# Kronecker feed-forward stage: how the eight PSUM banks are shared, where the output spreads stand in the order, and which queues store the last group

## The chip, the cores and the metric

The kernel runs on one NeuronCore of a Trainium2 chip. The metric is the device time of one execution in microseconds (us); the figure of a version is the median of its runs. All times inside the kernel come from one execution taken by the hardware profiler and are counted from its first instruction.

## The reference

The kernel computes two layers of a "metaformer" on an input of 4 x 32 x 32 tokens with 384 channels, all in fp32. The first layer (an attention and a mixture of experts) and the convolution of the second layer are not touched by the change. What matters is the last step, the feed-forward block of the second layer, whose two weight matrices are Kronecker products:

```python
def _L1_ffn_ref(x, c_fc_1, c_fc_2, c_proj_1, c_proj_2):
    w_fc = jnp.kron(c_fc_1, c_fc_2)          # (1536 x 32) kron (1 x 12)
    w_proj = jnp.kron(c_proj_1, c_proj_2)    # (32 x 1536) kron (12 x 1)
    h = x @ w_fc.T
    h = jax.nn.gelu(h, approximate=False)
    out = h @ w_proj.T
    return out
...
t = t + _L1_ffn_ref(_ln_t(t), ...)
```

Because of the Kronecker form, the 384 channels of a token shrink to 32 sums over 12 channels each, these 32 become 1536 hidden values, Gelu is applied, the 1536 values become 32 again, and each of the 32 is spread over 12 channels with the weights `c_proj_2`. The result is added to the input of the block.

## The kernel before

The 4096 tokens are 32 tiles of 128 tokens. The class `Kron` works on groups of 16 tiles (`GT`), so there are two groups, g = 0 and g = 1. The hidden values are 12 blocks (`NF`, f = 0 to 11) of 128. `shrink` (VectorE) makes the 32 sums of each token, and `run` (L1979) does the rest. In `run`:

- `turn(g)` (L1992) transposes the 32 sums of the 16 tiles on TensorE, so that 128 partitions hold four sets q of 32 rows and 512 columns hold four blocks n of 128 tokens. The tile of a pair (n, q) is 4n + q. VectorE copies the result out of PSUM (L2000).
- `hidden(g, f)`, called **H(f)** below, makes four matmuls (L2007), one for each q. Each contracts 32 rows, so the four stand on different 32-row strips of the array. Each writes its own PSUM tile `ps_h` of one bank (128 x 512 fp32), and ScalarE applies Gelu to each (L2012), which gives four tiles `h` in SBUF. In the trace every fp32 matmul is two weight loads and two matmul records, so H(f) shows as x8.
- `back(g, f)`, called **B(f)** below, makes four matmuls (L2018), one for each q, with all 128 rows and 32 columns each. They add into the four quarters of one PSUM bank `ps_y`. After f = 11 VectorE copies `ps_y` to `yT` (L2024).
- `spread(g, n, q)`, called a **spread** below, makes one matmul (L2031) with 32 rows that spreads the 32 values of 128 tokens over 384 channels into one PSUM bank `ps_o`. VectorE adds the input of the block (L2036) and writes a tile `o`, and a DMA of 192 KB stores it to `out` (L2037, issued by SyncE, SP). The tiles `o` rotate through four buffers.

The eight banks of PSUM are divided as four for `ps_h`, one for `ps_y` and three for `ps_o`, where `turn` uses the `ps_o` banks too. A matmul that writes a rotating tile waits until the reader of the tile that last held the bank is done.

The order of the work is written in the loop at the end of `run`. For each f it is H(f), then B(f-1); in group 0 also `begin` and `shrink` for group 1 and, at f = 10, `turn(1)`. In group 1, for f = 2 to 9, two spreads of group 0 follow B(f-1), so the sixteen spreads of group 0 lie inside the loop of group 1. The sixteen spreads of group 1 come after B(11), at the end of the program. In this part the framework orders the instructions of TensorE, VectorE and ScalarE by their place in the program and by what is ready in its own estimate; in the trace of before, TensorE's order in `run` is the order of the text. After the stage the program ends with a branch on the value `unsafe` (L2161) and a closing exchange of all engines.

Of the kernel before, what the change touches and what calls it, by code (L numbers as in the profile page):

```python
# [10 lines left out]
FP = mybir.dt.float32  # L11
# [3 lines left out]
PSUM = bass.MemoryType.PSUM  # L15

P = 128
# [1897 lines left out]
class Kron:  # L1915
# [63 lines left out]
    def run(self, out):  # L1979
        nc, tc, A = self.nc, self.tc, self.A  # L1980
        NG_ = NT // self.GT
        with ExitStack() as ctx:
            hp = ctx.enter_context(tc.tile_pool(name="kf_h", bufs=10, reuse_waits="tile"))
            tp = ctx.enter_context(tc.tile_pool(name="kf_t", bufs=2, reuse_waits="tile"))
            op = ctx.enter_context(tc.tile_pool(name="kf_o", bufs=4, reuse_waits="tile"))
            ps_h = ctx.enter_context(tc.tile_pool(name="kf_ps_h", bufs=4, space=PSUM, reuse_waits="tile"))
            ps_y = ctx.enter_context(tc.tile_pool(name="kf_ps_y", bufs=1, space=PSUM, reuse_waits="tile"))
            ps_o = ctx.enter_context(tc.tile_pool(name="kf_ps_o", bufs=3, space=PSUM, reuse_waits="tile"))
            xrT, hs, py = [], {}, {}
            yT = {}  # L1990

            def turn(g):  # L1992
                ps = ps_o.tile([P, 512], FP, name="ps_x", tag="o")
                flat = self.xr[g].rearrange("p t a -> p (t a)")
                for n in range(self.QT):
                    nc.tensor.transpose(
                        ps[:, n * P : (n + 1) * P], flat[:, n * P : (n + 1) * P], self.net.ident
                    )
                t = tp.tile([P, 512], FP, name="xrT", tag="xrT")
                nc.vector.tensor_copy(t, ps)  # L2000
                xrT.append(t)

            def hidden(g, f):
                for q in range(4):
                    rows = slice(A * q, A * q + A)
                    ps = ps_h.tile([P, 512], FP, name="ps_h", tag="h")
                    nc.tensor.matmul(  # L2007
                        ps, lhsT=self.wf[rows, f * P : (f + 1) * P], rhs=xrT[g][rows, :],
                        start=True, stop=True,
                    )  # L2010
                    h = hs[g, f, q] = hp.tile([P, 512], FP, name="h", tag="h")
                    nc.scalar.activation(h, ps, AF.Gelu)  # L2012

            def back(g, f):
                if f == 0:
                    py[g] = ps_y.tile([P, 512], FP, name="ps_y", tag="y")
                for q in range(4):
                    nc.tensor.matmul(  # L2018
                        py[g][A * q : A * q + A, :], lhsT=self.wp[:, f, :], rhs=hs.pop((g, f, q)),
                        start=f == 0, stop=f == NF - 1, skip_group_check=True,  # L2020
                    )
                if f == NF - 1:
                    yT[g] = tp.tile([P, 512], FP, name="yT", tag="yT")
                    nc.vector.tensor_copy(yT[g], py[g])  # L2024

            def spread(g, n, q):

                rows = slice(A * q, A * q + A)
                i = g * self.GT + 4 * n + q
                ps = ps_o.tile([P, 512], FP, name="ps_o", tag="o")  # L2030
                nc.tensor.matmul(  # L2031
                    ps[:, :C], lhsT=yT[g][rows, n * P : (n + 1) * P],
                    rhs=self.wide[rows, :, :].rearrange("p a k -> p (a k)"), start=True, stop=True,
                )
                o = op.tile([P, C], FP, name="o", tag="o")
                nc.vector.tensor_tensor(o, ps[:, :C], self.net.x(i), ALU.add)  # L2036
                nc.sync.dma_start(out=out[i * P : (i + 1) * P, :], in_=o)  # L2037

            turn(0)
            for g in range(NG_):  # L2040
                for f in range(NF):
                    hidden(g, f)
                    if f:
                        back(g, f - 1)
                    elif g:
                        back(g - 1, NF - 1)
                    if g + 1 < NG_:
                        if f == 0:
                            self.begin(g + 1)
                        if 1 <= f < 9:  # L2050
                            self.shrink(g + 1, 2 * f - 2)
                            self.shrink(g + 1, 2 * f - 1)
                        if f == 10:
                            turn(g + 1)
                    if g and 2 <= f < 10:
                        for q in range(2):
                            spread(g - 1, (f - 2) // 2, 2 * (f % 2) + q)
            back(NG_ - 1, NF - 1)
            for n in range(self.QT):
                for q in range(4):  # L2060
                    spread(NG_ - 1, n, q)


def gates(net, psum, gate_w, gate_b):
# [170 lines left out]
```

## Time and profile before

| what | us |
|---|---|
| median of three runs | 2975.26 (2974.44 to 2985.27) |
| the profiled execution's own time | 2946.74 |
| its span, first to last instruction | 2945.0 |
| H of group 0, f = 0 starts at | 2850.76 |
| H of group 1, f = 0 starts at | 2887.63 |
| last B of group 1 done, `yT` copied from | 2924.43 |
| last add of the program (L2036) from | 2937.22 |

The profiled execution is 28.5 us below the median of the runs without a profile. Times within the trace are compared with each other; a difference found there is then carried over to the median.

How to read what follows: a line of the timeline has the start in us, the duration in us, the engine (PE is TensorE's matmul, PEld its weight load, DVE is VectorE, ACT is ScalarE, SP is SyncE), the line, the operation, what is written from what, the shapes and the count of merged instructions. A bracket at the end says how long that engine was idle before it, and what released it.

### The profile page before, as it was taken

How to read it: one execution, taken by the hardware profiler on the slowest of the kernel's cores; microseconds unless marked ns; L12 is line 12 of the kernel's file. 1: busy time of each engine (PE TensorE's matmuls, PEld its weight loads, DVE VectorE, ACT ScalarE, POOL GpSimd, SP SyncE). 2: the span in 40 equal slices, each digit the busy share in tenths (PEclk: the TensorE clock that was granted, in tenths of full speed). 3: DMA queues.
4: the chain of work that ended last, by engine and by line, in shares of the span. 5: the costliest groups of instructions: out<-in, count | busy, mean ns of one | idle time of the engine just before them, and what ended most of it. 6: DMA issues, size and time to landing. Idle time of an engine off the chain costs nothing. (4 is left out here: it accounts for less than half of the span.)

```text
span 2945.0 us, 36681 instructions
## 1 busy us (share of the span) xinstructions
PE 2778.0 (94%) x13236; PEld 1476.9 (50%) x13236; DVE 1349.3 (46%) x3714; ACT 1214.8 (41%) x2023; POOL 396.8 (13%) x499
## 2 busy tenths in 40 slices
PE   6989999999989998699999999999999998999988
PEld 4323333233323332167777777777777754444433
DVE  1366667676866688633000001111111147877642
ACT  3777767777767776321121121121121122122125
POOL 1000000120011003114111112212211102100000
PEclk9999999999999998799999999999999999999998
DMA  5133334322322232355445455556556437644432
GB/s 102 43 100 93 93 87 121 83 61 64 101 54 58 63 103 74 106 200 198 178 173 194 175 188 210 195 208 216 193 211 213 144 132 236 191 156 160 144 104 88
DMA packets 216992, 405.91 MB, mean 138 GB/s; under 512 B 83505, under 2 KB 177905, under 8 KB 203745
## 3 DMA queue, kind: packets, MB, share of 16 engines
q1 hardware_dynamic: 186656, 190.77, 21.8%
q0 software_dynamic: 27152, 209.66, 20.8%
q10 hardware_dynamic: 2992, 3.03, 0.3%
q8 instruction: 107, 1.75, 0.3%
q14 instruction: 85, 0.69, 0.1%
HBM read 305.35 MB, written 49.99 MB: 121 GB/s over the span
## 5 line engine op out<-in xcount | busy, mean ns | idle before, releaser
L1611 ACT ACTIVATE h<-ps_h,up 128x256 f32<-128x256 f32 x420 | 198.5, 473 | 915.6 <-PE ps_h L1607 915.6
L1607 PE MATMUL ps_h<-xbT,up 128*128 128x256 f32 x2520 | 553.1, 380 | 2.6 <-ACT h L1611 1.8
L1624 PE MATMUL ps_y<-down,h 128*128 128x384 f32 x1680 | 554.9, 488 | 0.0
L1607 PEld LDWEIGHTS ps_h<-xbT,up 128*128 128x128 f32 x2520 | 480.3, 191 | 77.1 <-ACT h L1611 2.7
L686 DVE CUSTOM_DVE_ANT_0 e<-e,rz,inv 128x1024 f32<-128x1024 f32 x384 | 474.4, 1272 | 67.9 <-DMA rz<-r_row 65.0
L627 ACT ACTIVATE e<-ps_s,shift 128x1024 f32<-128x1024 f32 x384 | 407.1, 1109 | 117.0 <-PE ps_s L617 99.7
L1624 PEld LDWEIGHTS ps_y<-down,h 128*128 128x128 f32 x1680 | 317.9, 191 | 206.7 <-issue 1.5
L1629 DVE TENSOR_TENSOR y<-ps_y,down 128x384 f32<-128x384 f32 x70 | 39.0, 558 | 717.8 <-PE ps_y L1624 717.8
L635 PE MATMUL ps_z<-e,rt_ones 128*32 128x512 f32 x1536 | 271.9, 632 | 41.0 <-ACT e L627 41.0
L635 PE MATMUL ps_o<-e,wv 128*32 128x512 f32 x1536 | 215.2, 633 | 36.6 <-DVE wv L693 27.5
L617 PE MATMUL ps_s<-q,k 32*128 32x512 f32 x1536 | 233.2, 677 | 0.0
L713 POOL DMA_DIRECT2D q<-po x96 | 76.2, 874 | 989.5 <-DMA q<-po 588.2
L367 ACT ACTIVATE below<-tk_left,tk_bound 128x1024 bf16<-128x1024 f32 (+1 forms) x160 | 184.0, 1150 | 37.8 <-DVE tk_bound L373 16.5
L1735 PE MATMUL ps_a<-wa,xnT 128*128 128x486 f32 x384 | 167.6, 585 | 8.6 <-DVE attn L1745 6.8
L617 PEld LDWEIGHTS ps_s<-q,k 32*128 32x128 f32 x1536 | 63.6, 193 | 172.2 <-issue 170.5
L282 PE MATMUL ps_t<-xnT,wqkv 128*128 128x512 f32 x288 | 137.1, 617 | 7.1 <-ACT xnT L463 5.1
L635 PEld LDWEIGHTS ps_z<-e,rt_ones 128*32 128x32 f32 x1536 | 42.6, 110 | 187.6 <-ACT e L627 115.9
L635 PEld LDWEIGHTS ps_o<-e,wv 128*32 128x32 f32 x1536 | 31.2, 111 | 196.9 <-issue 71.6
L1735 PEld LDWEIGHTS ps_a<-wa,xnT 128*128 128x128 f32 x384 | 72.0, 193 | 93.5 <-issue 84.6
L1576 DVE SCALAR_TENSOR_TENSOR x<-yt,weight,x 128x384 f32<-128x384 f32 x38 | 23.5, 618 | 188.7 <-DMA x<-x 188.0
L1837 PE MATMUL ps_y<-band,v 128*32 128x194 f32 (+2 forms) x960 | 102.7, 517 | 7.4 <-DMA band<-room 7.2
L1490 POOL DMA_INDIRECT yt<-yg,index x64 | 66.7, 1042 | 305.5 <-DVE x L1576 142.8
(342 smaller groups left out, 2856.4 us busy)
## 6 DMA issues: line engine op xcount, KB each, us to landing
band<-room SPq DMA_DIRECT2D x32, 1560.0 KB
rz<-r_row SPq DMA_DIRECT2D x48, 512.0 KB
yg<-y SPq DMA_DIRECT2D x70, 192.0 KB
q<-q SPq DMA_DIRECT2D x192, 64.0 KB
k<-k SPq DMA_DIRECT2D x192, 64.0 KB
room<-none SPq DMA_DIRECT2D x64, 192.0 KB
x<-x SPq DMA_DIRECT2D x38, 192.0 KB
o<-in_x_dram SPq DMA_DIRECT2D x33, 192.0 KB
```

The costliest lines, as they stand in the source:

```text
L282: nc.tensor.matmul(ps, lhsT=lhsT(k), rhs=rhs(k), start=k == 0, stop=k == KC - 1)
L367: nc.scalar.activation(junk[:n], left[:n], AF.Sign, bias=bound[:n], accum_out=over[:n])
L617: nc.tensor.matmul(ps[:, half * 512 : half * 512 + 512], lhsT=self.k4[r, u * P : (u + 1) * P], rhs=self.q4[r, :], start=True, stop=True,)
L627: nc.scalar.activation(e, ps, AF.Exp, bias=shift, scale=QK_SCALE)
L635: nc.tensor.matmul(ps[r : r + 32, :], lhsT=lhsT(odd), rhs=self.es[2 * u + odd][:, half * 512 : half * 512 + 512], start=u == 0, stop=u == ...
L686: nc.vector.tensor_tensor_reduce(self.es[m], self.es[m], self.rz, 1.0, self.im["inv"][:, m, self.h : self.h + 1], ALU.mult, ALU.add, self. ...
L713: nc.gpsimd.dma_start(out=there, in_=po[r : r + 32, :], accum_op=ALU.add)
L1607: nc.tensor.matmul(ps, lhsT=up[:, o : o + P], rhs=xbT[:, k, :], start=k == 0, stop=k == KC - 1,)
L1611: nc.scalar.activation(h, ps, AF.Gelu, bias=up[:, KC * HID + f : KC * HID + f + 1])
L1624: nc.tensor.matmul(ps, lhsT=hs[f][:, t * P : (t + 1) * P], rhs=down[:, f * C : (f + 1) * C], start=f == 0, stop=f == NF - 1,)
L1735: nc.tensor.matmul(pa[:, hh, :HW_], lhsT=xnT[:, k, :], rhs=wa[:, k, hh * HW_ : (hh + 1) * HW_], start=k == 0, stop=k == KC - 1,)
L1837: nc.tensor.matmul(ys[c][32 * n : 32 * n + 32, lo - 512 * half : hi - 512 * half], lhsT=vs[b, t][:, h * HD : (h + 1) * HD], rhs=bands[b, t ...
```

## The change

The PSUM pools become six banks for `ps_h`, one for `ps_y` and one for `ps_o`. The two spreads that followed B(f-1) in group 1 are split: one now stands between H(f) and B(f-1), the other stays behind B(f-1). Call them **S_A(f)**, with q = 0 or 2, and **S_B(f)**, with q = 1 or 3. In the last group the spreads take their PSUM tile from the `ps_h` pool. Their stores are issued in turn by SP (even q) and by ScalarE's queue (odd q). The number of instructions of each kind stays the same.

```diff
-            ps_h = ctx.enter_context(tc.tile_pool(name="kf_ps_h", bufs=4, space=PSUM, reuse_waits="tile"))
+            ps_h = ctx.enter_context(tc.tile_pool(name="kf_ps_h", bufs=6, space=PSUM, reuse_waits="tile"))
             ps_y = ctx.enter_context(tc.tile_pool(name="kf_ps_y", bufs=1, space=PSUM, reuse_waits="tile"))
-            ps_o = ctx.enter_context(tc.tile_pool(name="kf_ps_o", bufs=3, space=PSUM, reuse_waits="tile"))
+            ps_o = ctx.enter_context(tc.tile_pool(name="kf_ps_o", bufs=1, space=PSUM, reuse_waits="tile"))
...
-            def spread(g, n, q):
+            def spread(g, n, q, queue=nc.sync):
...
-                ps = ps_o.tile([P, 512], FP, name="ps_o", tag="o")
+                if g < NG_ - 1:
+                    ps = ps_o.tile([P, 512], FP, name="ps_o", tag="o")
+                else:
+                    ps = ps_h.tile([P, 512], FP, name="ps_h", tag="h")
...
-                nc.sync.dma_start(out=out[i * P : (i + 1) * P, :], in_=o)
+                queue.dma_start(out=out[i * P : (i + 1) * P, :], in_=o)
...
                     hidden(g, f)
+                    if g and 2 <= f < 10:
+                        spread(g - 1, (f - 2) // 2, 2 * (f % 2))
                     if f:
                         back(g, f - 1)
...
                     if g and 2 <= f < 10:
-                        for q in range(2):
-                            spread(g - 1, (f - 2) // 2, 2 * (f % 2) + q)
+                        spread(g - 1, (f - 2) // 2, 2 * (f % 2) + 1)
             back(NG_ - 1, NF - 1)
             for n in range(self.QT):
                 for q in range(4):
-                    spread(NG_ - 1, n, q)
+                    spread(NG_ - 1, n, q, (nc.sync, nc.scalar)[q % 2])
```

## The prediction

> **What bounds the kernel now.** I read the head of the page first, for what share of the span the change can touch.
>
> ```profile
> span 2945.0 us, 36681 instructions
> ...
> PE 2778.0 (94%) x13236; PEld 1476.9 (50%) x13236; DVE 1349.3 (46%) x3714; ACT 1214.8 (41%) x2023; POOL 396.8 (13%) x499
> ```
>
> The average says "TensorE", but it is an average over stages. The change lives in the last 94.3 us (2850.7 to 2945.0), 3.2% of the span. So I read busy time by stretches (stretch and length; busy us and count of PE, PEld, DVE, ACT, POOL; clock; DMA share; GB/s):
>
> ```profile
> 2850.70:2885.50 34.80, 32.66 (x172) 11.32 (x172) 5.30 (x23) 25.66 (x47) 0.00 (x0) 0.90 0.00 0
> ...
> 2895.20:2919.00 23.80, 23.80 (x161) 8.59 (x160) 8.18 (x16) 16.45 (x33) 0.00 (x0) 1.00 0.33 116
> ...
> 2924.40:2937.90 13.50, 11.29 (x32) 5.89 (x32) 9.41 (x17) 0.00 (x0) 0.00 (x0) 0.68 0.60 214
> 2937.90:2945.00 7.10, 0.00 (x0) 0.00 (x0) 0.00 (x0) 0.00 (x0) 0.00 (x0) 0.50 0.15 50
> ```
>
> In the first two the PE looks full, yet ACT is idle a quarter of the time. At the end neither PE nor DVE is full, and the last 7.1 us hold only the branch and the closing exchange. The waits of this stage (total us, times, longest) say who holds whom:
>
> ```profile
> ACT h L2012 <- PE ps_h L2007: 27.7, 13, 8.9
> ...
> PEld ps_h L2007 <- ACT h L2012: 17.6, 36, 2.3
> ...
> PEld ps_o L2031 <- DVE o L2036: 7.0, 11, 1.3
> ```
>
> H and Gelu wait for each other. The timeline of group 0 shows how:
>
> ```profile
> 2869.01 1.14 PE L2007 MATMUL ps_h<-xrT,wf 32*128 32x512 f32 x8
> ...
> 2870.08 1.07 PE L2018 MATMUL ps_y<-h,wp 128*32 128x512 f32 x8
> 2870.16 4.13 ACT L2012 ACTIVATE h<-ps_h 128x512 f32<-128x512 f32 x8 [1.20 <-PE ps_h L2007]
> ...
> 2871.79 0.29 PEld L2007 LDWEIGHTS ps_h<-xrT,wf 32*128 32x128 f32 x2 [0.20 <-ACT h L2012]
> 2872.28 0.29 PEld L2007 LDWEIGHTS ps_h<-xrT,wf 32*128 32x128 f32 x2 [0.20 <-ACT h L2012]
> 2873.33 0.16 PEld L2018 LDWEIGHTS ps_y<-h,wp 128*32 128x32 f32 x8 [0.76 <-issue]
> ...
> 2874.33 1.14 PE L2007 MATMUL ps_h<-xrT,wf 32*128 32x512 f32 x8
> ```
>
> An unhindered H takes 1.07 us (2869.01 to 2870.08), B takes 0.99 (to 2871.07). The next H gets its third and fourth bank only as Gelu empties them (2871.79, 2872.28) and takes 2.26. Two f cost 5.33 us, while ACT works 4.13 and waits 1.20. The third place is the spread, inside group 1 and at the end:
>
> ```profile
> 2896.20 0.59 PE L2031 MATMUL ps_o<-wide,yT 32*128 32x384 f32 x2
> ...
> 2897.15 1.02 DVE L2036 TENSOR_TENSOR o<-ps_o,x 128x384 f32<-128x384 f32 x2 [5.44 <-PE ps_o L2031]
> ...
> 2926.12 2.12 DVE L2036 TENSOR_TENSOR o<-ps_o,x 128x384 f32<-128x384 f32 x4 [1.00 <-PE ps_o L2031]
> 2926.74 0.29 PEld L2031 LDWEIGHTS ps_o<-wide,yT 32*128 32x128 f32 x2 [1.25 <-DVE o L2036]
> ...
> 2930.35 1.73 DVE L2036 TENSOR_TENSOR o<-ps_o,x 128x384 f32<-128x384 f32 x3 [0.57 <-DMA out_dram<-o]
> 2932.64 1.73 DVE L2036 TENSOR_TENSOR o<-ps_o,x 128x384 f32<-128x384 f32 x3 [0.56 <-PE ps_o L2031]
> ```
>
> From a spread's start to its add: 0.95 us. From the add's start to the bank's next load: 2926.12 to 2926.74, 0.62. Two spreads with an H take 1.71 (2896.20 to the next B at 2897.91) instead of H's 1.07, because they hold two strips while H begins on the others.
>
> **What the Trainium skill says.** "Perfetto Trace Analysis", section Matmuls: independent matmul groups should rotate through PSUM banks so that emptying one overlaps the next. The 17.6 us of H waiting for Gelu agree; a single bank for spreads goes against it. "TensorEngine Tiling (Array Packing)", Key Properties: tiles of the array work independently, but a change of tiling mode drains the array. Agrees: four H, 8 records of some 0.6 us, fit into 1.14, and no B starts before its H is through. "DMA: Bandwidth & Descriptors", Issuing engines are not separate DMA queues: a second issuing engine saves only issue time. No stage here shows two queues storing at once. "TensorE: Matmul & The Clock Gate", What's actually happening: the clock is halved after too idle a window of about 3.4 us. The clock columns (0.90, 0.68) agree.
>
> **The change part by part.** Times are against the profiled execution.
>
> *Six banks for H, steady part.* From H(4) of group 0 (2865.74) to H(2) of group 1 (2892.95) are ten f in 27.2 us, one `turn` of 0.6 included. With six banks H(f+1) finds two banks free and the other two are emptied while B(f-1) runs. What remains is a chain over two f: last Gelu of f-1, 0.13 to B (seen at the end: Gelu 2921.23 + 0.52, load 2921.88), B 0.99, H 1.07, 0.08 to ACT, four Gelus 2.07: 4.34, or 2.17 per f. Floor: 2.07, ACT's and PE's own work. Ceiling: today's 2.66. I take 2.17: 10 x 2.17 + 0.6 = 22.3, **-4.9** (-5.9 to -3).
>
> *First four f of group 0.* They are paced by two table loads of 1.28 us and a half-clock stretch. Two early matmuls save little: **-0.5** (0 to -3.5 if the clock isn't halved).
>
> *Spreads of group 0 in group 1.* S_A(f) stands behind H(f) and ahead of B(f-1), so B, S_B and the next H queue behind it, and its add and its SP store come earlier. DVE has nothing else in group 1 and the SP only stores, so these cost nothing. Should DVE be busy, its add would lengthen PE's wait one for one. The order is S_B(f), H(f+1), S_A(f+1), B(f). With one bank S_A(f+1) must wait for S_B(f)'s add: 0.95 + 0.62 = 1.57 after S_B began, where H alone would be through at 1.07. It then holds its strip for 0.86 (its record would end 0.92 after start; B may load 0.06 sooner, as it does after H), and B can't start before. Period 1.57 + 0.86 + 0.99 = **3.42** per f. S_B finds the bank free: S_A's add frees it 1.57 after S_A's start, B ends 1.85 after. Before, from H(2) at 2892.95 to B(9) at 2919.08: 26.1. After: H and S_A (0.96 + 0.86), B 0.99, seven periods 23.9, a last S_B with H 1.71: 28.4. **+2.3**. No operation in the trace waits so; below: PE gets past the wait, 2.70 per f, -2.7; above: both spreads expose the full 1.57, 2 x 1.57 + 0.99 = 4.13, +7.3.
>
> *The three f at the end of group 1* (B(9) to the copy of `yT`): paced by the last Gelus as before, **0**.
>
> *Last group's spreads.* From the first add to the last: 2926.12 to 2937.22, 11.1 us, at half clock mostly: three banks give three spreads in 2.29 (2930.35 to 2932.64). With six, PE is not late any more. Next late is the ring of four `o` tiles: an add may reuse its tile only after the store, and the fifth add came 2.55 after the first (2928.67 against 2926.12; 1.87 of it the store, by the chain of waits). So adds 0, 0.47, 0.94, 1.41, then every four 2.55: the sixteenth at 1.41 + 3 x 2.55 = 9.06, -2.0. SP's last store is now the fifteenth tile, 0.5 sooner again. Its 7.1 us to the end stay, and cover ACT's own later close: before, ACT closed from 2921 on, hidden by everything; its issue of 0.3 to 0.4 (L217, L222) and a close of about 3.2 fit. Without this cover 0.5 is lost. DMA needs about 0.55 per store (0.60 share at 214 GB/s is 357 GB/s full), under the 0.64 of the ring. **-2.5** (0 to -4.5, where adds follow each 0.47).
>
> Sum: -4.9 - 0.5 + 2.3 - 2.5 = **-5.6 us**. The profiled 2946.74 becomes 2941.1. The runs stand 28.5 us above it for reasons the trace doesn't show; carried over, 2975.26 becomes **2969.7**.
>
> **Rivals.**
> 1. *PE isn't held by the one bank* (S_A in H's shadow): +2.3 becomes -2.7, 2964.7. For: loads of independent strips overlap in the trace. Against: every load seen waiting for a bank held those behind it.
> 2. *The stores bound the end*: two queues disturb each other, landing grows, no gain of the 2.5: 2972.2. For: DMA share 0.60 already.
> 3. *The order isn't the text's*: the scheduler moves spreads, since one bank changes what it thinks ready; stalls eat the gain, 2975. Against: before kept the text's order on PE.
> 4. *Slower: the clock.* While S_A runs alone one strip of four works. If windows of group 1 count as idle, the clock halves there: spreads and B double, 0.95 + 0.86 + 0.99 = 2.80 more per f, x8 = +22, net +17, 2992. It decides where strip-time falls to that of the tail (four spreads in 2.55, 4 x 0.75 of 10.2, 29%). Against: one period holds H (3.8), two spreads (1.5), B on all strips (3.6), 65% of 13.7.
>
> **The numbers.** Forecast 0.58, rival 1 0.14, rival 2 0.13, rival 3 0.10, rival 4 0.05. A measurement of this kernel tells about 0.5% (15 us) from no change. Below 2960.4 lies only rival 1 with a full clock at the start and both floors: 0.03. Above 2990.1 most of rival 4: 0.04. Within: 0.93. The range 2961 to 2978 leaves out rival 4 and the corners; it takes in the bounds of the spreads and the scatter of the runs.
>
> **What would show it.** Right: H to H in group 0 at 2.1 to 2.2; in group 1 about 3.4 per f with spreads waiting for L2036; adds at the end in fours of 2.55 with the DMA as releaser. Wrong: 2.7 per f in group 1 (rival 1), a half clock there (4), an unchanged 11 us at the end (2).

## The result and the profile after

| | before | after |
|---|---|---|
| median of 20 runs each | 2977.62 us (2964.85 to 2991.07) | 2967.24 us (2961.74 to 2983.53) |
| ratio after/before | | 0.9972, 95% interval 0.9958 to 0.9985 |
| the stage: first H to the end of the span, in the profiled execution | 94.25 us | 88.99 us |

The ratio, with its interval, stands for 8.3 us less (4.5 to 12.5); the two medians differ by 10.4. Forecast were 5.6 us less, or 0.2%, and a time of 2969.7 in a range of 2961 to 2978; the measured 2967.24 lies in it. The profiled execution of after as a whole is longer than that of before (span 2981.8 against 2945.0), but it loses all of that ahead of the stage, where both run the same 35475 instructions: the first H starts 42.0 us later (2892.80 against 2850.76). So the two traces are compared from the first H on, and below from one mark of the stage to the next.

The stage of after by stretches (stretch and length; busy us and count of PE, PEld, DVE, ACT, POOL; clock; DMA share; GB/s): H(4) of group 0 to H(2) of group 1, from there to B(9), most of the last group's spreads, the close.

```profile
2907.43:2929.76 22.33, 22.33 (x168) 6.19 (x164) 1.38 (x2) 20.09 (x40) 0.00 (x0) 1.00 0.00 1
2929.76:2957.89 28.13, 28.13 (x172) 9.70 (x168) 8.93 (x16) 18.64 (x36) 0.00 (x0) 1.00 0.30 106
2963.30:2974.80 11.50, 8.66 (x32) 4.64 (x32) 8.56 (x16) 0.00 (x0) 0.00 (x0) 0.73 0.62 221
2974.80:2981.80 7.00, 0.00 (x0) 0.00 (x0) 0.56 (x1) 0.00 (x0) 0.00 (x0) 0.50 0.29 100
```

The first stretch took 27.21 us before; now ACT works for 20.1 of its 22.3. The second took 26.13 and is 2.0 longer, at full clock. And the last add now falls into the last seven microseconds. The waits of the stage (total us, times, longest):

```profile
ACT h L2012 <- PE ps_h L2007: 24.2, 17, 9.0
...
PEld ps_o L2034 <- DVE o L2039: 11.1, 15, 0.8
...
PEld ps_h L2007 <- ACT h L2012: 3.2, 4, 2.2
...
DVE o L2039 <- DMA out_dram<-o: 2.5, 5, 1.6
```

H's wait for Gelu's banks fell from 17.6 to 3.2 us. A new wait stands beside it: the loads of a spread wait for the add before it, 11.1 us in 15 waits. The timeline of group 0:

```profile
2911.84 1.14 PE L2007 MATMUL ps_h<-xrT,wf 32*128 32x512 f32 x8
...
2912.91 1.07 PE L2018 MATMUL ps_y<-h,wp 128*32 128x512 f32 x8
2913.06 4.13 ACT L2012 ACTIVATE h<-ps_h 128x512 f32<-128x512 f32 x8 [0.27 <-PE ps_h L2007]
...
2913.91 1.41 PE L2007 MATMUL ps_h<-xrT,wf 32*128 32x512 f32 x8
...
2916.24 1.14 PE L2007 MATMUL ps_h<-xrT,wf 32*128 32x512 f32 x8
```

From H to the H after the next is 4.40 us (2911.84 to 2916.24) where it was 5.33, and ACT waits 0.27 in that time, not 1.20. In group 1 the one bank sets the pace:

```profile
2932.46 0.18 PEld L2034 LDWEIGHTS ps_o<-wide,yT 32*128 32x128 f32 x1 [0.84 <-DVE o L2039]
...
2933.40 0.56 DVE L2039 TENSOR_TENSOR o<-ps_o,x 128x384 f32<-128x384 f32 x1 [1.28 <-PE ps_o L2034]
...
2934.01 0.29 PEld L2034 LDWEIGHTS ps_o<-wide,yT 32*128 32x128 f32 x2 [0.62 <-DVE o L2039]
...
2934.85 0.16 PEld L2018 LDWEIGHTS ps_y<-h,wp 128*32 128x32 f32 x8 [0.55 <-issue]
...
2935.85 0.18 PEld L2034 LDWEIGHTS ps_o<-wide,yT 32*128 32x128 f32 x1 [0.84 <-DVE o L2039]
```

S_B starts at 2932.46, its add at 2933.40, S_A gets the bank at 2934.01 (1.55 after S_B), B starts 0.84 later, and the next S_B at 2935.85: a period of 3.39. At the end, the adds (VectorE alone):

```profile
2965.00 1.95 DVE L2039 TENSOR_TENSOR o<-ps_h,x 128x384 f32<-128x384 f32 x4 [1.00 <-PE ps_h L2034]
2967.58 1.11 DVE L2039 TENSOR_TENSOR o<-ps_h,x 128x384 f32<-128x384 f32 x2 [0.63 <-PE ps_h L2034]
...
2976.32 0.56 DVE L2039 TENSOR_TENSOR o<-ps_h,x 128x384 f32<-128x384 f32 x1 [1.58 <-DMA out_dram<-o]
```

The fifth add comes 2.58 after the first, as expected, but the last one 11.32 after the first, not 9.06, and it waited 1.58 us for a store. Before it was 11.10. So the end of the program became shorter although its adds did not. The chain of work that leads to this last add passes through three landings of stores (start and length):

```profile
2966.98 2.59 DMA out_dram<-o
...
2970.28 1.90 DMA out_dram<-o
...
2972.90 3.30 DMA out_dram<-o
```

An add may start only when the store four before it has landed. The forecast had put 1.87 us on each of these landings.

### The profile page after: what moved, and what is told of

It reads as the page before. It is cut to its first block, busy times and chain, and to the rows that moved or that the text cites. A ratio compares the mean times of both kernels' runs of the same rounds, so it can differ in the third digit from the quotient of the medians.

```text
span 2981.8 us, 36722 instructions
## 1 busy us (share of the span) xinstructions
PE 2787.8 (93%) x13236; PEld 1475.2 (49%) x13236; DVE 1349.0 (45%) x3714; ACT 1215.5 (41%) x2023; POOL 393.3 (13%) x499
```

## The experiments

Each is one profiled execution, apart from the last version, which was timed in six. Whole times of single runs scatter by ten microseconds and more (see the ranges above): five and two banks took 2977.42 us where the kernel before took 2972.42 beside it, though its stage is 7 us shorter. So each run is read from the sections of the stage. The marks are the first H, H(4) of group 0, H(2) of group 1, B(9) of group 1, the last copy of `yT` and the end of the span.

| run | H to H(4) | to H(2) | to B(9) | to `yT` | to the end | stage | first to last add | half clock at the start |
|---|---|---|---|---|---|---|---|---|
| before | 14.98 | 27.21 | 26.13 | 5.36 | 20.57 | 94.25 | 11.10 | 6.83 |
| after | 14.63 | 22.33 | 28.13 | 5.42 | 18.49 | 88.99 | 11.32 | 6.83 |
| spreads together | 12.99 | 22.61 | 35.34 | 5.42 | 18.47 | 94.82 | 11.32 | 3.41 |
| five and two banks | 15.06 | 24.48 | 23.33 | 5.42 | 18.94 | 87.23 | 11.67 | 6.83 |
| one queue (SP) | 13.00 | 22.61 | 28.13 | 5.42 | 22.25 | 91.41 | 12.01 | 3.41 |
| branch held | 14.43 | 22.34 | 28.13 | 5.42 | 18.18 | 88.49 | 9.92 | 6.83 |
| branch held, SP only | 14.41 | 22.51 | 28.13 | 5.42 | 19.40 | 89.86 | 10.00 | 6.83 |
| before, two queues | 15.32 | 27.03 | 26.13 | 5.36 | 18.46 | 92.30 | 10.97 | 10.24 |
| queues exchanged | 13.01 | 22.61 | 28.13 | 5.41 | 19.03 | 88.20 | 11.19 | 3.41 |
| ACT's queue only | 14.47 | 22.33 | 28.13 | 5.41 | 18.39 | 88.73 | 11.30 | 6.83 |
| eight tiles `o` | 12.99 | 22.61 | 28.13 | 5.41 | 15.79 | 84.93 | 7.14 | 3.41 |
| seven shared banks | 11.09 | 22.02 | 23.33 | 5.42 | 18.39 | 80.25 | 11.02 | 6.83 |
| seven banks, eight `o` | 9.03 | 22.02 | 23.33 | 5.42 | 16.14 | 75.95 | 7.24 | 0 |
| transposes in the H pool | 12.61 | 22.59 | 28.13 | 5.42 | 18.33 | 87.09 | 11.22 | 10.24 |

The first column must be read with the last one, which is the time for which TensorE was granted half its clock in that section. It differs between executions of otherwise equal code. In runs with the banks and the order of after, that section is 13.0 at 3.41 us (four runs) and 14.4 to 14.6 at 6.83.

**Is it the one bank that holds TensorE in group 1?** First, both spreads behind B, with the same banks:

```diff
-                    if g and 2 <= f < 10:
-                        spread(g - 1, (f - 2) // 2, 2 * (f % 2))
                     if f:
...
-                        spread(g - 1, (f - 2) // 2, 2 * (f % 2) + 1)
+                        for q in range(2):
+                            spread(g - 1, (f - 2) // 2, 2 * (f % 2) + q)
```

> The changed kernel with the two spreads of group 0 together behind B again, as in the kernel before, banks 6/1/1 kept. The stage (first H to the end of the span) took 89.0 us in the changed kernel, 94.2 before; in group 1 an f took 3.39. Theory (a load that waits for the one spread bank holds everything behind it on TensorE): the second spread waits 1.57 us after the first and H and B queue behind it, 1.57 + 0.75 + 0.96 + 0.1 + 0.99, about 4.3 per f, stage 96, slower than before. Rival (TensorE gets past the waiting spread, so the split is worth nothing): 3.4 per f or less, stage 89.

The weight loads of two f in its timeline:

```profile
2922.14 0.29 PEld L2034 LDWEIGHTS ps_o<-wide,yT 32*128 32x128 f32 x2 [0.84 <-issue]
...
2922.57 0.51 PEld L2007 LDWEIGHTS ps_h<-xrT,wf 32*128 32x128 f32 x2
...
2923.70 0.18 PEld L2034 LDWEIGHTS ps_o<-wide,yT 32*128 32x128 f32 x1 [0.62 <-DVE o L2039]
...
2925.40 0.16 PEld L2018 LDWEIGHTS ps_y<-h,wp 128*32 128x32 f32 x8 [0.76 <-issue]
...
2926.39 0.18 PEld L2034 LDWEIGHTS ps_o<-wide,yT 32*128 32x128 f32 x1 [0.84 <-issue]
```

The second spread starts 1.56 after the first (2922.14 to 2923.70), and everything behind it starts after it; a single matmul of H stands between the two. The period is 4.25 per f, and the section is 7.2 us longer than after's. So a load that waits for its bank holds what is behind it: no load of H, whose matmuls stand on the other strips too, passes it in the trace between 2923.08 and 2923.70. Then the other direction, a second bank for the spreads at the cost of one of H's:

```diff
-            ps_h = ctx.enter_context(tc.tile_pool(name="kf_ps_h", bufs=6, space=PSUM, reuse_waits="tile"))
+            ps_h = ctx.enter_context(tc.tile_pool(name="kf_ps_h", bufs=5, space=PSUM, reuse_waits="tile"))
...
-            ps_o = ctx.enter_context(tc.tile_pool(name="kf_ps_o", bufs=1, space=PSUM, reuse_waits="tile"))
+            ps_o = ctx.enter_context(tc.tile_pool(name="kf_ps_o", bufs=2, space=PSUM, reuse_waits="tile"))
```

> The changed kernel with five banks for H and two for the spreads. Theory (in group 1 the one spread bank costs the wait for the add, in group 0 six banks buy the whole gain): group 1 falls from 3.39 to 2.70 per f, the wait of spreads for adds is gone there, group 0 rises from 2.23 to about 2.45 per f because H's fourth matmul waits for Gelu again; stage about 86.6. Rival (the spread's place between H and B is what costs, not the bank): group 1 stays at 3.2 or more per f, stage 91.

B to B in its group 1 (the loads of B, and of S_B after it):

```profile
2937.82 0.16 PEld L2018 LDWEIGHTS ps_y<-h,wp 128*32 128x32 f32 x8 [0.55 <-issue]
...
2938.81 0.18 PEld L2034 LDWEIGHTS ps_o<-wide,yT 32*128 32x128 f32 x1 [0.84 <-DVE o L2039]
...
2940.51 0.16 PEld L2018 LDWEIGHTS ps_y<-h,wp 128*32 128x32 f32 x8 [0.55 <-issue]
```

2.70 per f instead of 3.39: the section falls from 28.13 to 23.33, below the 26.13 of before. With five banks H pays 2.15 us in group 0 (24.48 against 22.33), nearly half of what six banks had won. Over both sections five and two banks are 2.65 us shorter than six and one.

**Where does the gain at the end come from?** The prediction gave it to the six banks. So I took the second queue away, and in another run held TensorE's last branch back until the last add, since in the trace of after TensorE reaches that branch 8.91 us after the copy of `yT`, before it 11.71.

```diff
-                    spread(NG_ - 1, n, q, (nc.sync, nc.scalar)[q % 2])
+                    spread(NG_ - 1, n, q)
```

> The changed kernel with all stores of the last group on SP's queue. Theory A (the late stores at the end, 2.8 to 3.7 us instead of 1.9, stand behind the instruction fetch that TensorE's early branch starts, whichever queue issued them): stores issued after the fetch still land late, the last add stays about 11.3 us after the first, and SP now issues the last store itself, so the stage is some 2 us longer, 91. Theory B (two queues disturb each other): all stores land in about 1.9, the last add comes 9.1 after the first, stage about 88.8.

```diff
+            last = [None]
...
+                last[0] = o
                 queue.dma_start(out=out[i * P : (i + 1) * P, :], in_=o)
...
+            ps = ps_h.tile([P, 512], FP, name="ps_e", tag="h")
+            nc.tensor.matmul(ps[:A, :A], lhsT=last[0][:, :A], rhs=last[0][:, :A], start=True, stop=True)
```

> The changed kernel with one more small matmul at the end that reads the last output tile, so that TensorE reaches its branch only after the last add. Its result is not used. Theory A (TensorE's early fetch delays the stores): no store whose tile is used again lands later than 2.6, the last add comes 9.1 to 9.5 us after the first instead of 11.3, SP's last store about 0.6 sooner, stage about 88.3. Theory B (two queues disturb each other): the last stores still land after about 3.3 us and the last add comes 11.3 after the first.

With one queue the end is 22.25, 1.7 longer than before, in spite of six banks. Its last adds wait for a store that took 3.89 us to land (VectorE):

```profile
2965.94 0.56 DVE L2039 TENSOR_TENSOR o<-ps_h,x 128x384 f32<-128x384 f32 x1 [0.32 <-DVE o L2039]
2968.61 1.03 DVE L2039 TENSOR_TENSOR o<-ps_h,x 128x384 f32<-128x384 f32 x2 [2.11 <-DMA out_dram<-o]
```

With the branch held, no add after the first waits longer than 0.63 us (VectorE again):

```profile
2950.17 1.95 DVE L2040 TENSOR_TENSOR o<-ps_h,x 128x384 f32<-128x384 f32 x4 [1.00 <-PE ps_h L2035]
2952.74 1.71 DVE L2040 TENSOR_TENSOR o<-ps_h,x 128x384 f32<-128x384 f32 x3 [0.63 <-PE ps_h L2035]
2954.86 2.16 DVE L2040 TENSOR_TENSOR o<-ps_h,x 128x384 f32<-128x384 f32 x4 [0.42 <-DMA out_dram<-o]
2957.48 1.13 DVE L2040 TENSOR_TENSOR o<-ps_h,x 128x384 f32<-128x384 f32 x2 [0.46 <-DMA out_dram<-o]
2958.94 1.71 DVE L2040 TENSOR_TENSOR o<-ps_h,x 128x384 f32<-128x384 f32 x3 [0.33 <-DVE o L2040]
```

What changed on the DMA side is seen in the DMA queues of after, among them queues that bring instructions to the engines, between 2972.60 and 2976.30 (queue, packets, MB, share of 16 engines), where its slow stores lie:

```profile
q8 instruction: 1, 0.02, 1.8%
```

One packet of instructions of 16 KB takes 1.8% of 16 engines for 3.7 us, that is 1.07 us on one DMA engine. In all fourteen traces such a packet starts 0.9 to 2.4 us after TensorE's last branch. The trace counts the landing of a store in sixteen parts, and it shows that one late part holds a store back: of the store that the last add of after waits for (the twelfth of the group), fifteen parts landed 1.74 to 1.90 us after its issue and the last one after 3.30. It and the stores issued after it take 2.8 to 3.7 us to land. In the run with the branch held no such packet lies ahead of the last reused tile, all parts of the twelfth store landed within 1.89 us, and the last add starts 9.92 after the first. So the six banks let TensorE run ahead to the end of its work, instructions are fetched behind its branch while the stores still run, and the ring of four tiles `o` passes that on to the adds. That costs 1.4 us (11.32 against 9.92), and it took back what the banks had won.

Packets of 16 KB are not the only thing that makes a store late. With the branch held the last four stores, whose tiles no add needs, still took 2.85 to 3.12 us, each with one or two late parts, and ahead of the first of them lie only packets of 8 KB.

Yet holding the branch made the end only 0.3 us shorter. The reason is SP's closing list, the semaphore waits that SP runs through after its own last branch: one for each of the eight DMA semaphores, then for every engine's last sign. There it stood 1.2 us for VectorE and for TensorE's late branch. The hold pays its own gain back. The same hold with SP alone leaves a price for banks and ring without TensorE's fetch:

> The changed kernel with all last stores on SP's queue and the small matmul at the end that keeps TensorE from its branch until the last add (its result is not used). Between the copy of yT and the end of the span: 20.6 us before, 18.5 in the changed kernel, 22.3 with one queue and no hold. Theory (with one queue, the six banks at the end lose because TensorE's early instruction fetch delays stores that adds wait for): with the hold the last add comes 9.1 to 9.9 after the first instead of 12.0, and the stretch is about 19 to 19.5. Rival (one queue is too slow for these stores by itself): last add stays beyond 11, stretch 21 or more.

It ended at 19.40, 1.17 less than before. So with one queue six banks are worth 1.2 at the end without TensorE's fetch and -1.7 with it, and the second queue has to bring the rest. To see it alone, I gave the kernel before the second queue and nothing else:

```diff
-                    spread(NG_ - 1, n, q)
+                    spread(NG_ - 1, n, q, (nc.sync, nc.scalar)[q % 2])
```

> The kernel before with only the last group's stores split between SP's queue and ScalarE's. Theory (at the end the second queue takes the last store, and with it the late ones, off SP, on whose last store the end of the program hangs): adds as before, 11.1 from first to last, but SP's last store is the fifteenth tile, 1.1 us sooner; stage about 93. Rival (the second queue does nothing by itself; the banks did it): stage 94.2.

18.46, against 18.49 in after: the second queue alone gives the whole gain at the end, 2.1 us. It is not the adds (10.97 against 11.10), and it is more than the theory's 1.2 (94.2 to 93). Here is the close of six runs, in us after the copy of `yT`:

| run | stores issued by | SP's last issue | last landing | end | end after the landing |
|---|---|---|---|---|---|
| before | SP | 13.38 | 16.65 | 20.57 | 3.92 |
| one queue | SP | 14.28 | 17.14 | 22.25 | 5.11 |
| branch held, SP only | SP | 12.28 | 14.87 | 19.40 | 4.53 |
| after | SP, ACT | 11.46 | 16.57 | 18.49 | 1.92 |
| before, two queues | SP, ACT | 12.15 | 16.54 | 18.46 | 1.92 |
| five and two banks | SP, ACT | 11.66 | 17.02 | 18.94 | 1.92 |

In these three runs with two queues the program ends 1.92 after the last store has landed: nothing else is late. With SP alone it ends 2 to 3 us later than that. In SP's closing list, which waits for the eight DMA semaphores in turn, the kernel before has a gap of 1.72 us between two of them (at 3.54 and 1.82 before the end), though the store behind the second had landed some 8 us earlier. In that gap the DMA moved this and nothing else:

```profile
DMA packets 2, 0.02 MB, mean 9 GB/s; under 512 B 0, under 2 KB 0, under 8 KB 0
...
q14 instruction: 2, 0.02, 3.4%
```

Two packets of instructions of some 8 KB. SP's own waits in the kernel before (total us, times, longest) hold both its stalls, 2.8 right after its branch and the gap:

```profile
SPq L2161 <- SPq L2161: 4.5, 2, 2.8
```

The other two runs with SP alone have the same gap (1.90 and 1.70, with one and two such packets); none of the runs with stores on ACT has it. In six of these SP's list stands still for the last landing at about that place, which could cover a part of it; the other five wait there for at most 0.6 us. Whether SP's place (its last store comes one tile earlier) or its list without that fetch brings the gain, two runs told apart:

```diff
-                    spread(NG_ - 1, n, q, (nc.sync, nc.scalar)[q % 2])
+                    spread(NG_ - 1, n, q, (nc.scalar, nc.sync)[q % 2])
```

> The changed kernel with the two queues of the last group exchanged: ACT's queue stores the even q, SP the odd q, so that SP issues the sixteenth store. The question is why a second queue shortens the end. All times from the copy of the last yT. In the changed kernel the last store is issued at 13.61, lands 2.96 later, and the program ends 1.92 after that (18.49). In the kernel before, SP's last issue is at 13.38, the store lands at 16.66, yet the end comes at 20.57, 3.91 after the landing; in SP's closing list of waits there is a gap of 1.72 with two 8 KB instruction packets in it. Theory L: with half of the stores SP's instruction list is shorter and that fetch doesn't fall into its close, which then takes about 5.3 (in the run with seven banks 5.57, 0.34 of it waiting for a landing); the end is the later of the last landing + 1.92 and SP's last issue + 5.3: 18.5 to 19.0 here. Rival P: SP's close is a fixed 7.0 to 7.2, and the gain came from SP's last store being one tile earlier: 13.6 + 7.1 = 20.7.

```diff
-                    spread(NG_ - 1, n, q, (nc.sync, nc.scalar)[q % 2])
+                    spread(NG_ - 1, n, q, nc.scalar)
```

> The changed kernel with all sixteen stores of the last group on ACT's queue and none on SP's. Theory L (the end is the last landing + 1.92 once SP's close is short): last add as with SP alone, 12.0 after the first, so the last store at 14.3, landing about 3.0, end 19.2; if the late stores fall as in the changed kernel, 18.5. Rival D (two queues storing in turn is what gains, one queue of either kind is late): at least 20.6, up to the 22.25 of SP alone. Rival P (SP's last issue + 7.1) gives the same as L here; the run with the queues exchanged tells those two apart.

With SP issuing the sixteenth store at 13.47, later than in the kernel before, the end came at 19.03: SP's close took 5.56 and had no gap. Of SP's own waits only the one after its branch is left:

```profile
SPq L2165 <- SPq L2165: 2.9, 1, 2.9
```

The rival's 20.7 fails, but SP's place is worth something: here SP's close, not the last landing, ends the program, 0.54 us later than in after. With all stores on ACT's queue the end came at 18.39, again 1.92 after the last landing, and the adds were as late as with two queues (11.30). So the second queue as such does not count. Most of the gain is the missing gap: by estimate, the kernel before would end at 18.85 without its 1.72, and the other 0.4 us to 18.46 are SP's earlier last store. The gap is gone wherever SP issues fewer stores ahead of its closing list. "DMA: Bandwidth & Descriptors", section Issuing engines are not separate DMA queues, says that a second issuing engine saves no more than the time to issue; for the stores themselves these runs agree (18.39 with one queue, 18.49 with two).

**Is the ring of four the pace of the adds, and can the banks be shared?**

```diff
-            op = ctx.enter_context(tc.tile_pool(name="kf_o", bufs=4, reuse_waits="tile"))
+            op = ctx.enter_context(tc.tile_pool(name="kf_o", bufs=8, reuse_waits="tile"))
```

> The changed kernel with eight buffers for the output tiles instead of four. Theory (after the change the end is paced by the ring: an add waits for the landing of the store four before it, 2.6 us per four adds): no add waits for a store, adds follow each other by 0.47 to 0.56, the sixteenth about 7.5 to 8.5 after the first instead of 11.3, SP's last store about 1.5 to 2 us sooner, stage about 87. Rival (the transfers themselves are the bound): adds still stand at 0.64 or more and the stage stays near 89.

Its sixteen adds are one row of VectorE's timeline:

```profile
2925.17 7.68 DVE L2039 TENSOR_TENSOR o<-ps_h,x 128x384 f32<-128x384 f32 x16 [1.00 <-PE ps_h L2034]
```

The view shows no wait between them. The last starts 7.14 after the first, and the end is 15.79, 2.7 shorter. The stores land in 1.9 us at first and in up to 4.6 at last, but no add needs the tiles of the last eight any more. (The stage is 4.1 shorter; the rest is the shorter half clock of its first section.) Then one pool of seven banks for H, spreads and transposes:

```diff
-            ps_h = ctx.enter_context(tc.tile_pool(name="kf_ps_h", bufs=6, space=PSUM, reuse_waits="tile"))
+            ps_h = ctx.enter_context(tc.tile_pool(name="kf_ps_h", bufs=7, space=PSUM, reuse_waits="tile"))
...
-            ps_o = ctx.enter_context(tc.tile_pool(name="kf_ps_o", bufs=1, space=PSUM, reuse_waits="tile"))
...
-                ps = ps_o.tile([P, 512], FP, name="ps_x", tag="o")
+                ps = ps_h.tile([P, 512], FP, name="ps_x", tag="h")
...
-                if g < NG_ - 1:
-                    ps = ps_o.tile([P, 512], FP, name="ps_o", tag="o")
-                else:
-                    ps = ps_h.tile([P, 512], FP, name="ps_h", tag="h")
+                ps = ps_h.tile([P, 512], FP, name="ps_o", tag="h")
```

> The changed kernel with one pool of seven PSUM banks for H, the spreads and the transposes, the order of the text kept. Theory (what the one spread bank costs in group 1 is given back without taking banks from H in group 0): 2.2 per f in group 0, 2.70 per f in group 1, no wait of spreads for adds there, stage about 84.5 (89.0 minus 7 times 0.69). Rival (in a common ring the H of the next f meets banks that Gelu or an add still holds): group 1 at 3.0 or more per f, stage 87 or more.

Group 1 runs at 2.70 per f as with five and two banks, and group 0 is not slower than with six (22.02): H and the spreads don't need their banks at the same time. The first section is 3.5 us shorter as well, for another reason: the framework now put the square root of `begin(1)` ahead of the first Gelu, which saves one of the two table loads of 1.28 us on ACT. The first H starts 1.05 later for it, so 2.5 of the 3.5 remain. To see whether the transposes' tiles alone do that, I moved only those into H's pool:

```diff
-                ps = ps_o.tile([P, 512], FP, name="ps_x", tag="o")
+                ps = ps_h.tile([P, 512], FP, name="ps_x", tag="h")
```

> The changed kernel with only the transposes' PSUM tiles taken from the pool of H. In this order of instructions the square root of group 1 stands ahead of the first Gelu on ScalarE, not behind the fourth, as also in the two kernels with seven common banks. Theory (that, and not the banks, made the first four f of those kernels shorter): counted from the last add of L1857 ahead of the stage, H(4) starts 13.3 us later or less, where the changed kernel has 15.8; everything behind H(4) stays as in the changed kernel, 22.3, 28.1, 5.4 and 18.5. Rival (the seven banks or the clock did it): about 15.8 again, or 14.2 with the shorter half-clock stretch.

They do change the order: the square root came first here too, and the first H 1.05 later. From the last add of L1857 ahead of the stage to H(4) it took 14.86 us, against 15.83 in after and 13.3 expected. But the half clock lasted 10.24 us here against 6.83, so the size of this gain stays open between 1 and 2.5.

Both together, seven shared banks and eight tiles `o`, made the best version:

> Both together: seven common banks and eight output buffers, stores of the last group from both queues. Theory: the two savings add up, stage about 82.5, which is 6 to 7 us below the changed kernel and 12 below the one before; in the ratio to the kernel before about 0.996. Rival (one saving hides the other): stage 84 or more.

2927.72 us, median of 6, against 2948.22 of the kernel before in runs beside it (median of 11); ratio 0.9931, 95% interval 0.9908 to 0.9953. Its stage is 75.95 us. The two middle sections are those of seven shared banks, and among the last adds only the fourteenth waits, 0.17 us for a store (VectorE):

```profile
2919.54 6.13 DVE L2035 TENSOR_TENSOR o<-ps_o,x 128x384 f32<-128x384 f32 x13 [1.00 <-PE ps_o L2030]
2925.84 1.50 DVE L2035 TENSOR_TENSOR o<-ps_o,x 128x384 f32<-128x384 f32 x3 [0.17 <-DMA out_dram<-o]
```

Of the 18.3 us that its stage gained, at most 6 lie in the first section, where one execution without any half clock flatters it; the measured ratio, which stands for 20.3 us (13.9 to 27.1), agrees with the whole.

## Why the prediction was right, and where it was wrong

| step | forecast | measured in the stage |
|---|---|---|
| ten f of group 0 with six banks | -4.9 | -4.88 (27.21 to 22.33) |
| first four f | -0.5 | -0.35 (both with 6.83 of half clock) |
| spreads of group 0 in group 1 | +2.3 | +2.00 (26.13 to 28.13) |
| end of group 1 | 0 | +0.06 |
| last group's spreads and close | -2.5 | -2.08 (20.57 to 18.49) |
| sum | -5.6 | -5.26 |

**Group 0** went by its working: 2.17 per f from the chain Gelu, B, H, Gelu was forecast, and (22.33 - 0.6) / 10 is 2.17. The rows of before had all four links, and nothing else came late. Two small differences cancel: in the rows of after two f take 4.40, 2.20 each, and the `turn` then costs 0.3, not 0.6. With five banks the ten f took 24.48, between four (27.21) and six (22.33), so it is the banks that count here.

**The spreads** too: 3.42 per f from the hand-over of the bank, 3.39 measured. The hand-over was 1.55 instead of 1.57, and B came 0.84 after S_A's start, not 0.86. The runs with spreads together (4.25) and with two banks (2.70) show that it is the bank: one more hand-over on the path, or none, with the rest unchanged. Rival 1 (TensorE isn't held) falls with both. Rival 4 (the clock halves in group 1) falls with the clock column, 1.00 in that stretch. Rival 3 (another order) is not what happened in after; it did happen where the two spreads stand together, by one matmul of H, and for the square root with the shared pool.

**The end** is the step that failed, though its sum came near. "With six, PE is not late any more ... the sixteenth at 1.41 + 3 x 2.55 = 9.06, -2.0": the last add came at 11.32, 0.2 later than before. The ring's part of it held (a fifth add at 2.58, all adds unhindered with eight tiles), but TensorE, no longer late, went to its branch 2.8 us earlier, and stores around the instruction packet landed up to 1.8 later. With the branch held the last add came at 9.92. The 0.86 still missing to 9.06 lie mostly in the fourth store of the group: the working gave every store the 1.87 of the first, but the fourth, issued 0.47 behind the third, took 2.59, so the eighth add came at 4.70 and not at 3.96; two more turns of the ring took 2.6 each. The trace of before already had this in its third and fourth store (2.34 and 2.40). In after one of the fourth store's sixteen parts is 0.5 late, with an 8 KB instruction packet beside it; in the run with ACT's queue only there is no such packet, and that store took 2.05. "Its 7.1 us to the end stay": they did not. Before, 1.72 of them were the gap in SP's list, which is gone where SP issues fewer stores. SP's last issue to the end is 7.03 in after by chance: its list waited 1.76 there for ACT's last store. The end is now set by that landing, 16.57 + 1.92. So the term of -2.0 for banks is about 0 and the term of -0.5 for the close is about -2.1. Two numbers of the right total were put down to the wrong causes: that the sum came near was luck. That ACT's own close is covered was right, narrowly: ACT reported 0.28 us before SP did (1.10 and 0.82 before the end).

**Rival 2** had named its sign, an unchanged 11 us at the end, and that sign came. It had the place right (stores come late at the end, and they bound it now), but not the mechanism: the two queues don't disturb each other. In the kernel before the slowest store took 4.04 with one queue and 3.90 with two; in the changed kernel 3.89 with SP's alone, 3.72 with ACT's alone and 3.65 with both.

One reading of the prediction is loose: "no B starts before its H is through". B's first record starts 0.07 us before the last of H ends (2870.08 against 2869.01 + 1.14), so these rows show little overlap but not a drain.

The ratio stands for about 8 us where the stage gained 5.3; the interval (4.5 to 12.5) holds both. Whether the 3 us between them are more than scatter can't be told from these runs. That the gap in SP's list is a fetch, and why it comes with sixteen stores of the last group on SP and not with eight or none, is argued from the packets, not shown: nothing was run that moves the list alone.

## What to carry to other kernels

Before banks are split into pools, ask whether their users need them at the same time. One pool of seven gave H what six gave and the spreads what two gave; a pool of one bank costs the whole hand-over (matmul, add, next load: 1.55 us here) each time two users follow each other, and everything behind the waiting load pays it. "Perfetto Trace Analysis", section Matmuls, tells to rotate independent groups through banks; not doing so cost 3.39 against 2.70 us per f here.

At the end of a program, price the close by its own list: the last store's landing, each engine's last branch, and instruction packets among both. An engine that is made faster there reaches its branch sooner, and its fetch then runs among the stores that are still open. Where a ring of buffers paces the stores, look at the ring first: at this place eight tiles instead of four were worth more (2.7 us) than the banks (1.2 at best), and the late landings held almost no add back any more.

## What the runs showed of the hardware that I had not expected

- A packet of instructions of 16 KB took 1.07 us of one DMA engine in after (0.9 to 1.6 in all runs), and of the store of 192 KB that it met, one part of sixteen landed 1.4 us behind the others (3.30 us after the issue, where 1.9 is usual).
- SP's closing list stalls 1.7 to 1.9 us with instruction packets in the gap in all three runs in which SP issues all sixteen last stores, and in none of the eleven others (in six of those a wait for the last landing could cover a part).
- The half-clock stretch in the section from the first H to H(4) lasts 0, 3.41, 6.83 or 10.24 us, in steps of 3.41, from one execution to the next. "TensorE: Matmul & The Clock Gate", What's actually happening, gives a free-running window of 3413 ns, and the steps agree. Nearly the same instructions at the same place met none of them in one run (seven banks, eight `o`) and three in another (transposes in the H pool).
- ACT's change between Gelu and the square root costs 1.28 us each way and nothing beside it: in after Gelu ends at 2896.02, the table load starts at 2896.04, and the square root at 2897.34.
- With eight tiles thirteen stores of 192 KB were issued one every 0.465 us, 423 GB/s, with only the landing getting later (1.9 to 3.2 us for those that landed ahead of the 16 KB packet).
